# Graph attention, layer 0: edge weights as the stationary operand, features and factor in 65 moving columns, a bank of PSUM for each tile of nodes

## The chip, the cores and the metric

The kernel runs on one core of a Trainium2 chip. The metric is the time of one execution on the device in microseconds (us); the time of a kernel is the median of its runs. One more execution is taken with the hardware profiler, and all views of the profile come from that one.

## What is computed

Two layers on a graph of 3327 nodes with 256 features each. The change touches layer 0, an attention with 4 heads of 64 features:

```python
support = (inputs @ weight).reshape(n, H, OUT_F).transpose(1, 0, 2)
f1 = jnp.einsum('hno,ho->hn', support, weight_u[..., 0])
f2 = jnp.einsum('hno,ho->hn', support, weight_v[..., 0])
w = jax.nn.leaky_relu(f1[:, None, :] + f2[:, :, None], NEG_SLOPE)
e = jnp.where(mask, jnp.exp(neg - m), 0.0)      # mask: adj_mat != 0
attn = e / denom                                # denom: sum of e over the sources
out = jnp.einsum('hnm,hmo->hno', attn, support) + bias + inputs @ proj_w.T + proj_b
```

`inputs` is the input, normalized and cut off at zero; the result is added to the input. So each node gets, for each head, a weighted sum of the features of its sources (65 numbers: 64 features and the sum of the weights that they are divided by). Layer 1 then makes two steps with a dense attention of which only the largest probabilities are kept, and products with the adjacency; it is the longer part of the kernel and stays as it is but for small matters named below.

## The kernel before

All data are f32. The nodes are 26 tiles of 128 (the last has 127). The exponential of a leaky ReLU of a sum is written as a product: the weight from source m to target n is, up to a factor that cancels in the division, `max(cf[m], factor[n]) * adj[m, n]` times `eas[m]`, where `cf`, `eas` and `factor` are exponentials of f1 and f2 made once for each node.

Layer 0 goes over four **blocks** of target nodes (three of 8 tiles, that is 1024 nodes, and one of 255 nodes), and in each block over the 26 tiles j of sources: 104 **steps**. A step does this:

- SP loads a tile of the transposed adjacency `at` three steps ahead (`load_adj`), and POOL's queue stores it once more (`adj_r`, for layer 1).
- DVE makes the weights of each head in one instruction, `w = max(factor, cf) * at` (`weigh`, L560), 128 x 1024. Seven buffers of `w` lie between DVE and PE. The factors lie spread over all partitions, in the tiles `xf0` of layer 1's graph, which are free until then, and for the last block in `cb_end`.
- PE sums over the sources into PSUM. The features `sup` (already multiplied by `eas`) are the stationary operand, 64 columns for a head, and the weights `w` move, 512 columns to a matmul; two heads run side by side in two halves of the array (`sum_features`, L568). The sum of the weights is made apart, with `eas` broadcast to 32 stationary columns, four heads side by side (`sum_weights`, L578). For 1024 nodes that takes six banks of PSUM: two pairs of heads and the sums, each of 2 x 512 columns. An f32 matmul shows in the trace as two weight loads and two matmuls.

In block 0, PE also makes the features of tile j + 10 in step j, while there are any (`turn` L366: two transposes; `features` L377, L379, L381: f1, f2, and 512 columns of features and projection); the first ten tiles are made ahead of the loop. `take` (L410 to L417, DVE) multiplies the features by `eas`. `spread` writes the exponentials of f2 for four tiles at a time to memory and loads them back, broadcast to all partitions, on SP's queue.

At a block's end the six banks are copied to `ot` (L649, ACT and DVE in turn), targets in the columns. The tiles of a finished block (`Out`) then go through seven small stages beside the steps of the next block, three steps apart, listed by step in `on_pe` and `on_dve`: `divide` (L427, three transposes that bring the targets to the partitions), `normalize` (L435 to L454: the division, the residual in four instructions L441, the layer norm), `turn` L463, `keys` L473, `take_keys`, `graph` L496 and `take_graph` L507. Each takes one of the two banks that the sums leave free. The last block's tiles go through the same behind the loop, after the mean of the keys (L262).

The order of the instructions on PE, DVE, ACT and POOL is the order in which the program is written (`in_traced_order`). `load_graph` (L221) loads the graph's tiles from memory between the two steps of layer 1, on POOL's queue, four tiles to a load.

Of the kernel before, what the change touches and what calls it, by code (L numbers as in the profile page):

```python
# [21 lines left out]
P = 128  # L22
D = 256
DC = D // P
H = 4
# [29 lines left out]
def kernel(  # L55
# [25 lines left out]
    HB = 8  # L81

    def rows(i):
        return min(P, N - i * P)

# [84 lines left out]
    def hi_and_lo(qk, p, i, s):  # L170

        pn, at = rows(i), centres[:, s : s + 1]
        if i == 0:
            nc.vector.tensor_reduce(at[DA:], p[DA:, :32], AX.X, ALU.add)
            nc.vector.tensor_scalar(at[DA:], at[DA:], -1.0 / 32, None, ALU.mult)
        nc.scalar.activation(qk[:, 0, :pn], p[:, :pn], AF.Identity, bias=at)
        yield
        nc.vector.scalar_tensor_tensor(
            qk[:, 1, :pn], p[:, :pn], at, qk[:, 0, :pn].bitcast(FP), ALU.add, ALU.subtract
        )  # L180
# [25 lines left out]
    def new_graph(pool):  # L206


        return [
            pool.tile([P, min(HB, NT - c), 2 * DX - 2], FR, tag=f"xf{c}", name=f"xf{c}")  # L210
            for c in range(0, NT, HB)
        ]

    def ones_of_graph(xf, c0, c1):
        b = c0 // HB
        nc.gpsimd.tensor_copy(
            xf[b][:, c0 - b * HB : c1 - b * HB, D:DX],
            one.unsqueeze(2).to_broadcast([P, c1 - c0, DX - D]),
        )

    def load_graph(pool, s):  # L221
        xf = new_graph(pool)
        for g in range(0, NT, 4):
            b = g // HB
            if s == 0:
                ones_of_graph(xf, g, min(g + 4, NT))
            for t0, t1 in ((g, min(g + 4, NF)), (max(g, NF), min(g + 4, NT))):
                if t0 < t1:
                    n0, n1 = t0 * P, min(t1 * P, N)
                    p = min(P, n1 - n0)  # L230
                    for v in range(2):
                        move_rows(
                            nc.gpsimd,
                            xf[b][:, t0 - b * HB : t1 - b * HB, v * DX : v * DX + D].bitcast(FP),
                            xf_d[s][n0:n1, v].rearrange("(t p) d -> p t d", p=p), p,
                        )
        return xf
# [54 lines left out]
    with ExitStack() as l0:  # L292
# [38 lines left out]
        sup = p0.tile([P, NT, D], FP, name="sup")  # L331
        cf = p0.tile([P, NT, H], FP, name="cf")
        eas = p0.tile([P, NT, H], FP, name="eas")
# [5 lines left out]

        cb_end = p0.tile([P, H, N - (NT - 1) // HB * HB * P], FP, name="cb_end")  # L340
# [32 lines left out]
        def features(i, k):  # L373
# [8 lines left out]
            if i % 4 == 0:  # L382
                made["ef"] = pa.tile([H, 4, P], FP, tag="ef", name="ef", bufs=1)
            nc.scalar.activation(eas[:, i], f1, AF.Exp, scale=SLOPE)
            nc.scalar.activation(cf[:, i], f1, AF.Exp, scale=1.0 - SLOPE)
            nc.scalar.activation(made["ef"][:, i % 4], f2, AF.Exp, scale=SLOPE - 1.0)
            if i % 4 == 3 or i == NT - 1:
                spread(i // 4 * 4, i + 1, made["ef"])
            made[i] = pw

        def spread(t0, t1, ef):

            n0, n1 = t0 * P, min(t1 * P, N)
            nc.sync.dma_start(
                out=f2_d[:, n0:n1], in_=ef.rearrange("h t n -> h (t n)")[:, : n1 - n0]
            )
            b = t0 // HB
            for h in range(H):
                src = f2_d[h, n0:n1]
                if b == (NT - 1) // HB:  # L400
                    nc.sync.dma_start(out=cb_end[:, h], in_=src.partition_broadcast(P))
                else:
                    nc.sync.dma_start(
                        out=xf0[b][:, t0 - b * HB : t1 - b * HB, h * P : (h + 1) * P].bitcast(FP),
                        in_=src.partition_broadcast(P).rearrange("q (t n) -> q t n", n=P),
                    )

        def take(i):
            pw = made.pop(i)
            nc.vector.tensor_tensor(  # L410
                sup[:, i].rearrange("p (h o) -> p h o", h=H),
                pw[:, 0].rearrange("p (h o) -> p h o", h=H),
                eas[:, i].unsqueeze(2).to_broadcast([P, H, O]), ALU.mult,
# [6 lines left out]
        class Out:  # L420
            def __init__(r, i, ot, t0):
                r.i, r.pn, r.n0, r.ot, r.t0 = i, rows(i), i * P, ot, t0

            def divide(r, k):
                r.pt = bank(k, [P, HP + 1, P])
                for v in range(HP + 1):
                    nc.tensor.transpose(  # L427
                        r.pt[: r.pn, v, :], r.ot[:, v, r.t0 : r.t0 + r.pn], ident
                    )

            def normalize(r):
                pn, i, pt = r.pn, r.i, r.pt
                rden = small.tile([P, H], FP, tag="rden", name="rden")

                nc.vector.tensor_scalar(rden[:pn], pt[:pn, HP, ::QP], 1.0 / BIG, None, ALU.max)  # L435
                nc.vector.reciprocal(rden[:pn], rden[:pn])
                x1 = pa.tile([P, D], FP, tag="x1", name="x1")
                for h in range(H):
                    hs = slice(h * O, (h + 1) * O)
                    q0 = (h % 2) * O  # L440
                    nc.vector.scalar_tensor_tensor(  # L441
                        x1[:pn, hs], pt[:pn, h // 2, q0 : q0 + O], rden[:pn, h : h + 1],
                        res[:pn, i, hs], ALU.mult, ALU.add,
                    )
# [47 lines left out]
            def graph(r, k):  # L492
# [6 lines left out]
                nc.scalar.copy(xf0[i // HB][:pn, i % HB, :D], pu[:pn, 0])  # L499
# [4 lines left out]
            def take_graph(r):  # L504
                pn, n0, i = r.pn, r.n0, r.i
                xc = xf0[i // HB][:, i % HB]
# [10 lines left out]
        CH = HB * P  # L517
        HP = H // 2
# [32 lines left out]
        def weigh(j, at, b, cn, *heads):  # L551
            pj = rows(j)
            for h in heads:
                ws[h] = w = pa.tile([P, CH], FP, tag="w", name="w", bufs=7)
                if cn == CH:
                    cb = xf0[b][:pj, :, h * P : (h + 1) * P].bitcast(FP)
                    a, o = (t[:pj].rearrange("p (t n) -> p t n", n=P) for t in (at, w))
                else:
                    cb, a, o = cb_end[:pj, h], at[:pj, :cn], w[:pj, :cn]
                nc.vector.scalar_tensor_tensor(o, cb, cf[:pj, j, h : h + 1], a, ALU.max, ALU.mult)  # L560

        def sum_features(accs, j, p):
            pj = rows(j)
            for m, acc in enumerate(accs[p]):
                mn = min(512, cn - 512 * m)
                for q in range(2):
                    h = 2 * p + q
                    nc.tensor.matmul(  # L568
                        acc[q * O : (q + 1) * O, :mn], sup[:pj, j, h * O : (h + 1) * O],
                        ws[h][:pj, 512 * m : 512 * m + mn], start=(j == 0), stop=(j == NT - 1),  # L570
                    )

        def sum_weights(accs, j):
            pj = rows(j)
            for m, acc in enumerate(accs[HP]):
                mn = min(512, cn - 512 * m)
                for h in range(H):
                    nc.tensor.matmul(  # L578
                        acc[h * QP : (h + 1) * QP, :mn],
                        eas[:pj, j, h : h + 1].to_broadcast([pj, QP]),  # L580
                        ws[h][:pj, 512 * m : 512 * m + mn], start=(j == 0), stop=(j == NT - 1),
                    )
# [3 lines left out]
        def load_adj(b, j):  # L586
            c0, pj = b * CH, rows(j)
            cn = min(CH, N - c0)
# [3 lines left out]
        NB = (N + CH - 1) // CH  # L592
# [6 lines left out]
        for step, (b, j) in enumerate(order):  # L599
            c0 = b * CH  # L600
            cn = min(CH, N - c0)
            if j == 0:
                ws = {}
                half = range((cn + 511) // 512)
                accs = [[bank(len(half) * p + m, [P, 512]) for m in half] for p in range(HP + 1)]
# [17 lines left out]
            sum_features(accs, j, 0)  # L623
# [4 lines left out]
            sum_features(accs, j, 1)  # L628
            if b == 0 and i + 1 < NT:
                turn(i + 1, 6)  # L630
            sum_weights(accs, j)
# [12 lines left out]
            ot = pa.tile([P, HP + 1, CH], FP, tag="ot", name="ot", bufs=1)  # L644
            copies = (nc.scalar.copy, nc.vector.tensor_copy)
            for p in range(HP + 1):
                for m, acc in enumerate(accs[p]):
                    mn = min(512, cn - 512 * m)
                    copies[(p + m) % 2](ot[:, p, 512 * m : 512 * m + mn], acc[:, :mn])  # L649
# [3 lines left out]
            outs = [Out(c0 // P + t, ot, t * P) for t in range((cn + P - 1) // P)]  # L653
            if b < NB - 1:
                last = b == NB - 2
                for k, r in enumerate(outs):
                    a = step + 1 + 3 * k
                    ka, kb, kc = ((3, 4)[k % 2], (5, 6)[k % 2], 7) if last else (6, 7, 6)
                    g = a + 5
                    for when, f in (  # L660
                        (a, lambda r=r, ka=ka: r.divide(ka)),
                        (a + (3 if last else 2), lambda r=r, kb=kb: r.turn(kb)),
                        (a + (4 if last else 3), lambda r=r, kb=kb: r.keys(kb)),
                        (g, lambda r=r, kc=kc: r.graph(kc)),
                    ):
                        on_pe.setdefault(when, []).append(f)
                    for when, f in (
                        (a + 1, r.normalize),
                        (a + (5 if last else 4), r.take_keys),
                        (g + 1, r.take_graph),  # L670
# [3 lines left out]
        for k, r in enumerate(outs):  # L674
            r.divide(k)
# [6 lines left out]
        for k, r in enumerate(outs):  # L682
            r.graph(k)
            r.take_graph()

# [24 lines left out]
    def graph(i, s, xf, ends):  # L710
# [5 lines left out]
        for g in range(NG):  # L716
# [21 lines left out]
            for n, (w, c) in enumerate(todo):  # L738
                begin, end = g == 0 and n == 0, g == NG - 1 and n == len(todo) - 1
                xc = xf[c // HB][: rows(c), c % HB]  # L740
# [29 lines left out]
    class Rows:  # L770
# [54 lines left out]
        def guess(r):  # L825
# [31 lines left out]
            for j in (0, 2):  # L857
                g.tensor_scalar(r.at[:pn, j : j + 1], ssum, TOP_P * (1 - MARGIN), None, ALU.mult)
# [557 lines left out]
```

## Time and profile before

| | |
|---|---|
| time, median of 3 runs | 2210.81 us (2210.72 to 2212.17) |
| the profiled execution's own time | 2213.91 us |
| its span, first to last instruction | 2211.7 us |
| granted clock of TensorE, mean | 0.975 |
| PE busy | 2015.5 us, 91% of the span |
| PEld (weight loads) busy | 1394.6 us, 63% |
| DVE busy | 1690.6 us, 76% |
| ACT busy | 1297.6 us, 59% |
| POOL busy | 706.8 us, 32% |
| L560, weights on DVE | 312 instructions of 1277 ns on average |
| L568, sums of features on PE | 1456 rows, 342.5 us busy |
| L578, sums of weights on PE | 1456 rows, 166.5 us busy |

PE is TensorE's matmul, PEld its weight load, which runs beside it; DVE, ACT, POOL and SP are the vector, scalar, GpSimd and sync engines. A view of slices cuts the span into 40 equal parts, each digit being the busy share in tenths. Timelines give the start, the length, the engine, the line of the kernel, the operation, "output<-inputs", the shapes and the count of instructions that were merged into the row; in brackets stands the idle time before them and what ended it. Matmuls are pipelined and their ends are modelled, so the distance of two starts says more than a length. Groups give busy time and the mean length of one in ns.

### The profile page before, as it was taken

Reading aid. Unit: us, or ns where it says so; the run is one execution under the profiler, and the core shown is the slowest. Engines: PE = TensorE matmul, PEld = TensorE weight load, DVE = VectorE, ACT = ScalarE, POOL = GpSimd, SP = SyncE. Lnnn points to the kernel's source line nnn. Section 1 sums busy time; section 2 is a strip of 40 time slices with the busy share of each in tenths; the row PEclk is TensorE's granted clock in tenths of the full one; section 3 lists DMA queues with packets and bytes.
Section 4 is the critical chain, followed back from the end, with each engine's and each line's share of the span. In section 5 each row is a group of like instructions: output and inputs, shape, how many; then the busy total and the mean of one; then the engine's idle time right before and its main releaser. Section 6 shows DMA issues by size and latency. Waiting matters only on the chain. (4 is left out here: it accounts for less than half of the span.)

```text
span 2211.7 us, 34340 instructions
## 1 busy us (share of the span) xinstructions
PE 2015.5 (91%) x11474; PEld 1394.6 (63%) x11474; DVE 1690.6 (76%) x3996; ACT 1297.6 (59%) x2016; POOL 706.8 (32%) x1827
## 2 busy tenths in 40 slices
PE   6999999999997799999999999865999999999997
PEld 3333233233234678888878888754888888888886
DVE  4777888788784678777777777744788888888885
ACT  2110001001113978888888888718898899999982
POOL 2320133223232332222222222214444444444441
PEclk9999999999998799999999999988999999999998
DMA  5445465566454333333333333455333343433330
GB/s 170 147 168 181 164 199 190 190 210 205 152 171 135 83 82 92 95 95 96 96 91 96 96 94 95 115 153 163 84 94 100 94 103 96 112 97 96 93 81 19
DMA packets 319569, 270.60 MB, mean 122 GB/s; under 512 B 30168, under 2 KB 293335, under 8 KB 319256
## 3 DMA queue, kind: packets, MB, share of 16 engines
q1 hardware_dynamic: 303480, 216.03, 36.0%
q0 software_dynamic: 14736, 51.62, 6.5%
q8 instruction: 92, 1.51, 0.3%
q14 instruction: 93, 0.76, 0.1%
q10 hardware_dynamic: 1168, 0.67, 0.1%
HBM read 177.79 MB, written 88.62 MB: 120 GB/s over the span
## 5 line engine op out<-in xcount | busy, mean ns | idle before, releaser
L879 ACT ACTIVATE junk<-lg,at 128x3327 fp8e4<-128x3327 f32 (+1 forms) x208 | 637.9, 3067 | 5.0 <-POOL at L845 2.7
L560 DVE SCALAR_TENSOR_TENSOR w<-xf,cf,at 128x1024 f32<-128x1024 f32 (+1 forms) x312 | 382.0, 1277 | 56.4 <-PE pt L578 56.4
L741 PE MATMUL accr<-xf,adjt 128*128 128x258 f32 (+3 forms) x1352 | 365.9, 304 | 18.7 <-DMA adjt<-adj_r 18.5
L568 PE MATMUL pt<-w,sup 128*64 128x512 f32 (+3 forms) x1456 | 342.5, 579 | 10.4 <-DVE w L560 8.5
L742 PE MATMUL accr<-xf,adjt 128*128 128x256 f32 (+1 forms) x1352 | 339.5, 284 | 0.0
L1018 PE MATMUL acca<-res,wt 128*128 128x256 f32 (+2 forms) x1352 | 324.0, 382 | 0.6 <-ACT wt L1007 0.6
L1018 PE MATMUL acca<-xa,wt 128*128 128x256 f32 (+2 forms) x1352 | 316.4, 383 | 0.1
L997 PE MATMUL pt<-ident,e 128*128 128x128 f32 (+1 forms) x1352 | 208.3, 282 | 81.8 <-DVE e L984 52.4
L741 PEld LDWEIGHTS accr<-xf,adjt 128*128 128x128 f32 (+1 forms) x1352 | 259.7, 192 | 30.1 <-DMA adjt<-adj_r 19.9
L1018 PEld LDWEIGHTS acca<-xa,wt 128*128 128x128 f32 (+2 forms) x1352 | 252.1, 192 | 32.4 <-ACT wt L1007 0.5
L1018 PEld LDWEIGHTS acca<-res,wt 128*128 128x128 f32 (+2 forms) x1352 | 247.4, 192 | 30.1 <-ACT wt L1007 1.2
L742 PEld LDWEIGHTS accr<-xf,adjt 128*128 128x128 f32 (+1 forms) x1352 | 260.2, 192 | 4.6
L798 PE MATMUL pg<-k_sb,q 128*128 128x512 f32 (+2 forms) x728 | 237.4, 428 | 21.3 <-ACT lg L809 12.0
L997 PEld LDWEIGHTS pt<-ident,e 128*128 128x128 f32 (+1 forms) x1352 | 164.7, 146 | 144.7 <-ACT wt L1007 46.4
L819 POOL TENSOR_SCALAR sc<-sc 128x1 f32<-128x1 f32 (+1 forms) x156 | 30.8, 224 | 662.0 <-ACT sc L817 662.0
L568 PEld LDWEIGHTS pt<-w,sup 128*64 128x64 f32 (+1 forms) x1456 | 96.2, 136 | 222.3 <-issue 149.7
L945 DVE MAX8 v<-lg 128x8 f32<-128x416 f32 (+2 forms) x416 | 209.9, 577 | 0.0
L1007 ACT COPY wt<-pt 128x512 f32<-128x512 f32 (+3 forms) x286 | 148.1, 520 | 100.1 <-PE pt L997 93.2
L936 DVE SCALAR_TENSOR_TENSOR lg<-e,th 128x3327 f32<-128x3327 f32 (+1 forms) x52 | 191.1, 3675 | 2.2 <-ACT th L929 2.2
L984 DVE SCALAR_TENSOR_TENSOR e<-e,vm 128x3327 f32<-128x3327 f32 (+1 forms) x52 | 191.4, 3680 | 0.9
L821 ACT ACTIVATE e<-lg,sc 128x3327 f32<-128x3327 f32 (+1 forms) x52 | 159.8, 3074 | 25.2 <-PE pt L997 22.9
L578 PE MATMUL pt<-w,eas 128*32 128x512 f32 (+3 forms) x1456 | 166.5, 568 | 0.0
(179 smaller groups left out, 2615.5 us busy)
## 6 DMA issues: line engine op xcount, KB each, us to landing
adjt<-adj_r SPq DMA_DIRECT2D x300, 256.0 KB, 3.1
at<-in_adj_t_dram SPq DMA_DIRECT2D x75, 512.0 KB, 3.7
adj_r<-at POOLq DMA_DIRECT2D x75, 512.0 KB, 4.8
qk_d<-qk SPq DMA_DIRECT2D x50, 128.0 KB, 2.4
q<-qk_d SPq DMA_DIRECT2D x100, 64.0 KB, 2.4
xf_d<-xf SPq DMA_DIRECT2D x50, 128.0 KB, 2.8
xf_d<-hl SPq DMA_DIRECT2D x25, 256.0 KB, 2.1
xf<-f_d SPq DMA_DIRECT2D x24, 256.0 KB, 4.9
```

The costliest lines, as they stand in the source:

```text
L560: nc.vector.scalar_tensor_tensor(o, cb, cf[:pj, j, h : h + 1], a, ALU.max, ALU.mult)
L568: nc.tensor.matmul(acc[q * O : (q + 1) * O, :mn], sup[:pj, j, h * O : (h + 1) * O], ws[h][:pj, 512 * m : 512 * m + mn], start=(j == 0), st ...
L578: nc.tensor.matmul(acc[h * QP : (h + 1) * QP, :mn], eas[:pj, j, h : h + 1].to_broadcast([pj, QP]), ws[h][:pj, 512 * m : 512 * m + mn], sta ...
L741: nc.tensor.matmul(acc[:pn, :dx], w, xc[:, :dx], start=begin, stop=False)
L742: nc.tensor.matmul(acc[:pn, :D], w, xc[:, DX:], start=False, stop=end)
L798: nc.tensor.matmul(r.pg[p][:pn, :mn], r.q[:, v, :pn], k_sb[:, m0 : m0 + mn], start=(v == 0), stop=(v == 1),)
L879: nc.scalar.activation(junk[:pn], r.lg[:pn, :N], AF.Exp, bias=r.at[:pn, 4:], accum_out=r.g[:pn], saturate=False,)
L936: nc.vector.scalar_tensor_tensor(r.lg[:pn, :N], e, r.th[:pn], e, ALU.is_lt, ALU.mult, accum_out=r.below[:pn])
L945: nc.vector.max(r.v8[:pn, q], r.lg[:pn, q * w : min((q + 1) * w, N)])
L984: nc.vector.scalar_tensor_tensor(e, e, r.vm[:pn, 1:], e, ALU.is_ge, ALU.mult, accum_out=kept[:pn])
L997: nc.tensor.transpose(r.pt[g][: rows(c), j, : r.pn], r.e[: r.pn, c * P : c * P + rows(c)], ident[: r.pn, : r.pn],)
L1018: nc.tensor.matmul(r.acc[: r.pn], wt[: rows(c), j, : r.pn], xa[: rows(c), c, :], start=(c == 0), stop=(c == NT - 1),)
```

## The change

The operands of the sums change places. `w` becomes the stationary operand, 128 sources by 128 targets, and 65 columns move: the 64 features of the head and, as the 65th, `eas`. So the targets come out in the partitions, a bank of PSUM holds the 4 x 65 sums of one tile of targets, and neither the sums of the weights apart nor the transposes of `divide` are there any more. Six banks hold the sums of six tiles, so the blocks are now five: four of 6 tiles and one of two (`BLOCKS`), and what was spread and loaded four tiles at a time goes by three (`CHUNKS`).

```diff
-    HB = 8
+    BLOCKS = ((0, 6), (6, 12), (12, 18), (18, 24), (24, NT))
+    CHUNKS = tuple((t, min(t + 3, NT)) for t in range(0, NT, 3))
...
-        sup = p0.tile([P, NT, D], FP, name="sup")
+        sup = p0.tile([P, NT, H, O + 1], FP, name="sup")
...
-            nc.scalar.activation(eas[:, i], f1, AF.Exp, scale=SLOPE)
+            nc.scalar.activation(sup[:, i, :, O], f1, AF.Exp, scale=SLOPE)
...
+        def factors(b):
+
+            w = (BLOCKS[b][1] - BLOCKS[b][0]) * P
+            t = xf0[b].rearrange("p t d -> p (t d)")[:, : H * w]
+            return t.bitcast(FP).rearrange("p (h n) -> p h n", h=H)
...
-            def divide(r, k):
-                r.pt = bank(k, [P, HP + 1, P])
-                for v in range(HP + 1):
-                    nc.tensor.transpose(
-                        r.pt[: r.pn, v, :], r.ot[:, v, r.t0 : r.t0 + r.pn], ident
-                    )
...
-                for h in range(H):
-                    hs = slice(h * O, (h + 1) * O)
-                    q0 = (h % 2) * O
-                    nc.vector.scalar_tensor_tensor(
-                        x1[:pn, hs], pt[:pn, h // 2, q0 : q0 + O], rden[:pn, h : h + 1],
-                        res[:pn, i, hs], ALU.mult, ALU.add,
-                    )
+                nc.vector.tensor_tensor(
+                    x1[:pn].rearrange("p (h o) -> p h o", h=H), sums[:, :, :O],
+                    rden[:pn].unsqueeze(2).to_broadcast([pn, H, O]), ALU.mult,
+                )
+                nc.vector.tensor_add(x1[:pn], x1[:pn], res[:pn, i])
...
-        CH = HB * P
-        HP = H // 2
+
+        CH = max(t1 - t0 for t0, t1 in BLOCKS) * P
...
+                nc.vector.scalar_tensor_tensor(
+                    w[:pj, :cn], factors(b)[:pj, h, :cn], cf[:pj, j, h : h + 1], at[:pj, :cn],
+                    ALU.max, ALU.mult,
+                )
+
+        def sum_up(accs, j, cn, *heads):
+
             pj = rows(j)
+            for h in heads:
+                for t, acc in enumerate(accs):
+                    mn = min(P, cn - t * P)
                     nc.tensor.matmul(
+                        acc[:mn, h], ws[h][:pj, t * P : t * P + mn], sup[:pj, j, h],
+                        start=(j == 0 and h == 0), stop=(j == NT - 1 and h == H - 1),
                     )
...
-                accs = [[bank(len(half) * p + m, [P, 512]) for m in half] for p in range(HP + 1)]
+                accs = [bank(t, [P, H, O + 1]) for t in range(b1 - b0)]
...
-            sum_features(accs, j, 0)
+            sum_up(accs, j, cn, 0, 1)
             if b == 0 and i < NT:
                 features(i, 7)
             for f in on_pe.pop(step, ()):
                 f()
-            sum_features(accs, j, 1)
+            sum_up(accs, j, cn, 2)
             if b == 0 and i + 1 < NT:
                 turn(i + 1, 6)
-            sum_weights(accs, j)
+            sum_up(accs, j, cn, 3)
...
-            ot = pa.tile([P, HP + 1, CH], FP, tag="ot", name="ot", bufs=1)
+            outs = []
             copies = (nc.scalar.copy, nc.vector.tensor_copy)
...
+            for t, acc in enumerate(accs):
+                mn = min(P, cn - t * P)
+                sums = pa.tile([P, H, O + 1], FP, tag="ot", name="ot", bufs=CH // P)
+                copies[t % 2](sums[:mn], acc[:mn])
+                outs.append(Out(b0 + t, sums))
```

The stages of a finished tile are listed anew for six tiles to a block: normalize in the step where divide was, and the others one to two steps earlier than before. The graph's tiles `xf` follow the blocks of six, their loads the chunks of three. Two more small edits lie outside: the mean of the first keys is taken over 16 columns in place of 32 (`hi_and_lo`), and one of two constants in `guess` (POOL) is a little larger.

## The prediction

> **What bounds the kernel now.** I read the share of each engine in 40 slices first, since the change touches one stage only.
>
> ```profile
> PE   6999999999997799999999999865999999999997
> DVE  4777888788784678777777777744788888888885
> ```
>
> A slice is 55.3 us (2211.7 / 40). PE stands at 9 from the second to the twelfth, with DVE at 7 or 8: layer 0's sums end near 680 us, and PE looks like their bound. The stages say it more exactly. I cut the stretch at the starts of L560 (weights), which marks each block's first step, and at L262, after the last sums. Columns: length, then busy time and instructions of PE, PEld, DVE, ACT, POOL, clock, DMA share, GB/s.
>
> ```profile
> 52.40:254.10 201.70, 199.80 (x1055) 64.54 (x1054) 153.43 (x180) 20.58 (x81) 39.42 (x52) 0.99 0.51 165
> 254.10:429.50 175.40, 172.94 (x936) 53.24 (x936) 147.33 (x190) 15.58 (x41) 51.81 (x59) 0.99 0.59 195
> 429.50:604.20 174.70, 171.96 (x936) 53.20 (x936) 147.01 (x189) 16.79 (x45) 51.55 (x59) 1.00 0.55 182
> 604.20:683.80 79.60, 75.24 (x521) 30.12 (x522) 61.42 (x187) 16.54 (x45) 27.81 (x57) 1.00 0.54 162
> ```
>
> These 631.4 us are the four blocks before. PE is busy 99% in the first three, DVE 76 to 84%. The third view is PE's timeline over two plain steps of block 0:
>
> ```profile
> 209.87 3.65 PE L568 MATMUL pt<-w,sup 128*64 128x512 f32 x16
> 213.46 1.92 PE L578 MATMUL pt<-w,eas 128*32 128x512 f32 x16
> 215.31 3.65 PE L568 MATMUL pt<-w,sup 128*64 128x512 f32 x16
> ```
>
> A step takes 215.31 - 209.87 = 5.44 us. An f32 matmul shows as two rows (two passes). The 16 rows of L568 run in pairs (64 columns of the array each), those of L578 in fours, so the step is 8 + 4 = 12 passes of 512 columns at 0.43 us, or 5.15, and 0.3 for changing between the two shapes. DVE needs 4 x 1.196 = 4.78 of it (L560 start to start) and waits 0.57 for PE. So PE bounds, and DVE is 12% behind.
>
> **What a new pass costs.** The changed program holds 2704 matmuls of 65 moving columns (26 source tiles x 4 heads x 26 target tiles), so 5408 passes, each with its own load of 128 f32 columns of weights. No row has that pair; these enclose it (start, length of the whole run, count at the end):
>
> ```profile
> 30.04 0.53 PEld L377 LDWEIGHTS pt<-wuv,hT 128*128 128x128 f32 x4
> 1705.24 1.07 PE L997 MATMUL pt<-ident,e 128*128 128x128 f32 x8 [0.92 <-DVE e L984]
> 1700.15 1.89 PE L1018 MATMUL acca<-xa,wt 128*128 128x256 f32 x8
> ```
>
> - L377 moves 4 columns only. Four loads take 0.53, one alone 0.192 by its group: (0.53 - 0.19) / 3 = **0.112 us** a pass. So few columns stream for next to no time: this is the pace of a 128x128 f32 load.
> - L997 moves 128 columns behind the same load: (1.07 - 0.27) / 7 = 0.114, and 0.109 between starts inside the run.
> - L1018 moves 256: (1.89 - 0.38) / 7 = 0.216, which is the 0.43 us of 512 columns halved. The next load starts 2 ns after the matmul starts and adds nothing: load and matmul overlap, and the longer one sets the pace.
>
> 65 columns stream for 65/256 of 0.213 = 0.054 us, half of the load. So the pass waits for the load: I take 0.112, from L377, which has the same load and a stream shorter than it. From below 0.109 (L997). From above 0.118, the pace of L741/L742 (256 columns in 0.28-us rows that start 0.12 apart), where load and stream both take about 0.107 and get in each other's way.
>
> The page "TensorE: Matmul & The Clock Gate" of the Trainium skill, section "LDWEIGHTS (loading the stationary operand)", makes a load P / 1.2 ns for P columns, whatever the rows: 107 ns here, an estimate that speaks against the change and would make the passes 27 us cheaper in sum than mine. The same page's Part 3 says that a load overlaps matmuls in flight only where the row group differs; L1018's 0.216 has the same rows in both and shows overlap, so there the trace decides.
>
> **The sum, from 52.4 us to the end of the sums.**
> - Sums: 5408 x 0.112 = 606. Before: 26 x (3 x 5.44 + 1.77) = 470, 1.77 being the unladen step of 255 columns (609.22 to 610.99, starts of L560). So +136 on the path. A step of six tiles costs 48 x 0.112 = 5.4 us, as much as one of eight before: same price, a quarter fewer nodes.
> - Features in 16 steps of block 0: 8.94 - 5.44 = 3.50 before. Their passes alone make 4 x 0.112 + 4 x 0.109 + 4 x 0.43 + 2 x 0.109 = 2.8; without shape changes around them I put 3.0, so 48 and not 56.
> - The finished tiles that run beside the next block, 24 as before (four times six, three times eight), at turn 0.22 + keys 0.44 + graph 1.72 = 2.4, with gaps 2.6: 62. Before, divide (three transposes, 0.33) and shape changes around each made about 3.25: 78.
> - Block ends: DVE's copy of the last bank waits for PE's last pass, and the next block's L560 stand behind it in DVE's queue; PE waits for them. Copy about 0.4, one weight instruction of 768 columns 0.93 ((1.196 - 0.395) / 769 = 1.042 ns a column, from the 1024 and 255 rows), latencies 0.2, and about 1.1 more when normalize stands ahead of head 2: 2.6 x 4 = 10. Before, the step 13.42 us at 416.12 held the last graph and six copies of 0.6 to 0.7, some 6 more than a plain step: 19 for three.
> - Last block: PE 16 x 0.112 = 1.8 a step, DVE 1.58 and its share of the tiles' work; I add 4 for waits on both, against 8 before (laden steps took 9.17 in three, PE's own sum was 8.8, eight tiles).
> - Start and last copies: 2, as before less the flush of the last graph.
>
> 606 + 48 + 62 + 10 + 4 + 2 = 732 against 631: **+101 us**.
>
> Costed at nothing: DVE's 520 weight instructions in place of 416 (104 x (4 x 0.929 + 0.395) = 428 against 425 before) lie under PE, 3.7 in a 5.4 us step; without PE as cover they would be the bound, as in the first rival. The four L441 of 0.19 become two of 0.42 on DVE: +0.1 a tile, under PE. DMA moves the same bytes of adjacency in five pieces, in a longer stretch than the one at 165 to 195 GB/s. The spread of the factors issues nine groups of five on SP rather than seven; ACT's exponential into the single ef buffer waits for its store every third tile, with the copy of hT behind it, and PE for that: a store is 0.27 us of issue and some 2 to landing, features come 8 us apart in the loop, so only the opening can feel it: 0 to 2 us. Between the layers POOL issues four more loads of the graph; there each issue already waits about 1 us for the one ahead (340 GB/s), the bytes are equal, and I put 0, within 5 either way. Layer 1's plan stays as it is but for one constant on POOL, the same number of instructions.
>
> The profiled execution took 2213.9 (span 2211.7, 2.2 around it), so 2315 on its scale; it lies 3.1 above the median 2210.8, and 2210.8 + 101 = **2312**.
>
> **The rivals.**
> 1. *Faster: the pass goes at its 65 columns.* If loads of f32 weights came quicker than L377 shows, a pass would take 65/128 of 0.107 + 0.0025 = 0.057: 308 us in all, PE 420. DVE would bound: 428 + 84 (its 509 busy less 425) + about 25 of waits = 537, 94 less than 631: 2117. The sign turns at (606 - 101) / 5408 = 0.093 us a pass. For it: nothing loads f32 weights under a stream of 65 columns. Against: 104 passes of L377 with 4 columns, whose loads come no faster than 0.11.
> 2. *Slower by far: the load isn't hidden* behind so short a matmul: 0.112 + 0.054 = 0.166, +292: 2604. Against it: L1018 and L997 overlap.
> 3. *Load and stream disturb each other* as in L741/L742: 0.118, +32, and a wait of each head's first load for DVE of up to 0.03 (520 of them, 15): 2345 to 2360.
> 4. *The clock falls*, since the array streams half of the time only. Granted clock is 0.80 where PE is busy 70% (700 to 750 us) and 1.00 at 99%. With half the clock throughout it would be +600: about 2900. The loads keep PE occupied without gaps over 3 us, so I give it little.
>
> The page "TensorEngine Tiling (Array Packing)", section "Performance Considerations", advises to swap stationary and streaming where the RHS is at most 64 wide, together with column tiling; here the RHS is 65 wide and no columns are tiled, and no row shows that form.
>
> **How the numbers follow.** Forecast (0.109 to 0.114 and the small terms) 0.79; third rival 0.12; first 0.05; second 0.03; the fourth or something near no change 0.01. Bounds: 0.109 takes 16 off, the gaps in features and tiles another 10: 2285. 0.118 and the heads' waits add 47: 2360. What lies outside is some 0.1 to 0.2. Within 0.2%, about what measurement can tell from no change, I put 0.01; faster 0.05; slower 0.94.
>
> **What would show it.** PE at 9 in all slices up to some 780 us. The new rows' loads 0.11 apart, 48 passes in 5.4 us. Plain steps of block 0 near 5.4, laden ones 8.4. DVE waiting on PE between steps, longer than 0.57. No three transposes a tile. I'm wrong if loads come under 0.093 apart, if steps show DVE back to back, or if the clock drops there.

## The result, and the profile after

The changed kernel takes 2384.28 us (median of 4 runs, 2382.59 to 2386.07) against 2211.21 for the kernel before: 1.0782 times as long, 95% interval 1.0764 to 1.0801. That is 173 us slower where 101 were forecast, and 24 above the upper end of the range. The profiled execution spans 2384.2 us against 2211.7.

The page of the changed kernel, its slices of 59.6 us:

```profile
PE   6999999999999977999999999986699999999987
DVE  4667477477477746787777777784588888888885
...
PEclk9999599599599788999999999998799999999998
```

The clock of the kernel before, in its slices of 55.3 us:

```profile
PEclk9999999999998799999999999988999999999998
```

PE is busy for longer, up to the fourteenth slice, as forecast. The line that was not forecast is the clock: before, it stood at 9 in the first twelve slices, up to 663 us of layer 0's 684; now it falls to 5 three times, once after the start of each of blocks 1 to 3, and to 7 in the last block. DVE's dips to 4 lie in the three slices of 5. The blocks (from the first weight instruction of each to the next, and the last up to the mean of the keys) show how much; columns as in the prediction:

```profile
51.30:244.50 193.20, 191.71 (x1472) 170.18 (x1470) 125.34 (x181) 19.91 (x81) 35.48 (x51) 0.97 0.42 136
244.50:422.70 178.20, 176.71 (x1308) 169.40 (x1308) 114.43 (x157) 12.64 (x33) 39.64 (x51) 0.87 0.45 147
422.70:600.90 178.20, 176.61 (x1308) 169.81 (x1308) 114.31 (x157) 12.57 (x33) 39.12 (x51) 0.87 0.44 144
600.90:780.70 179.80, 178.27 (x1308) 171.01 (x1308) 114.33 (x157) 12.57 (x33) 39.66 (x51) 0.86 0.42 136
780.70:857.00 76.30, 73.73 (x476) 66.33 (x476) 57.52 (x155) 11.46 (x31) 24.31 (x50) 0.82 0.49 149
```

These are 805.7 us against 631.4: +174, all of the difference. What lies behind them, layer 1 with the four more loads of its graph, takes 1527 against 1528 us (mean of the keys to the end).

Within block 1 the clock is at a half for 47.8 us and full for the rest:

```profile
247.40:295.20 47.80, 47.80 (x214) 45.57 (x214) 22.20 (x32) 1.94 (x4) 10.89 (x13) 0.50 0.32 109
295.20:422.70 127.50, 127.14 (x1082) 122.03 (x1081) 89.43 (x120) 10.70 (x29) 28.75 (x38) 1.00 0.51 164
```

PE's timeline at the start and at the end of that stretch says what stands there:

```profile
241.81 2.17 PE L563 MATMUL pt<-sup,w 127*128 127x65 f32 x18
245.64 2.70 PE L563 MATMUL pt<-sup,w 128*128 128x65 f32 x19 [1.65 <-DVE w L552]
```

```profile
271.08 20.58 PE L563 MATMUL pt<-sup,w 128*128 128x65 f32 x96
291.46 3.72 PE L493 MATMUL pt<-ug,hT 128*128 128x512 f32 x4
294.97 0.48 PE L460 MATMUL pt<-ident,res 128*128 128x128 f32 x2
295.29 4.91 PE L563 MATMUL pt<-sup,w 128*128 128x65 f32 x43
```

Ahead of the stretch lies the end of a block: PE's last pass starts at 243.7, and the next block's first at 245.6, since DVE must copy a bank and then make weights. In the stretch 96 passes take 20.4 us from start to start (291.46 less 271.08), 0.212 each. It ends with the first matmuls of 512 columns, the first finished tile's graph product in step 4; behind them a pass takes (4.91 - 0.28) / 42 = 0.110. All together, the record of the granted clock has 184 us at half clock in these blocks (10.2, 47.8, 47.8, 51.2, 27.3) and 6.8 in the blocks before the change. Each of these stretches is a whole number of 3.4 us, called a window from here on. Half of the added 177 is 89 us, more than the 72 that were missing from the forecast.

### The profile page after: what moved, and what is told of

Same layout as the page of the kernel before. It is cut to its first block, busy times and chain, and to the rows that moved or that the text cites. A ratio compares the mean times of both kernels' runs of the same rounds, so it can differ in the third digit from the quotient of the medians.

```text
span 2384.2 us, 39418 instructions
## 1 busy us (share of the span) xinstructions
PE 2190.6 (92%) x13892; PEld 1939.3 (81%) x13892; DVE 1706.8 (72%) x4051; ACT 1296.6 (54%) x2018; POOL 716.8 (30%) x1858
## 5 line engine op out<-in xcount | busy, mean ns | idle before, releaser
L563 PEld LDWEIGHTS pt<-sup,w 128*128 128x128 f32 (+2 forms) x5408 | 689.0, 211 | 19.1 <-issue 15.2
L563 PE MATMUL pt<-sup,w 128*128 128x65 f32 (+2 forms) x5408 | 690.3, 294 | 8.3 <-DVE w L552 8.3
L552 DVE SCALAR_TENSOR_TENSOR w<-xf,cf,at 128x768 f32<-128x768 f32 (+2 forms) x520 | 442.6, 904 | 58.0 <-PE pt L563 57.8
L783 PEld LDWEIGHTS pg<-k_sb,q 128*128 128x128 f32 (+1 forms) x728 | 126.0, 194 | 43.8 <-ACT lg L794 16.3
```

What stands on the lines that cost most here:

```text
L552: nc.vector.scalar_tensor_tensor(w[:pj, :cn], factors(b)[:pj, h, :cn], cf[:pj, j, h : h + 1], at[:pj, :cn], ALU.max, ALU.mult,)
L563: nc.tensor.matmul(acc[:mn, h], ws[h][:pj, t * P : t * P + mn], sup[:pj, j, h], start=(j == 0 and h == 0), stop=(j == NT - 1 and h == H - 1),)
L783: nc.tensor.matmul(r.pg[p][:pn, :mn], r.q[:, v, :pn], k_sb[:, m0 : m0 + mn], start=(v == 0), stop=(v == 1),)
```

## The experiments

The theory, made from these lines: the idle time at a block's end halves the clock. The stream of 65 columns, in which the array works only 0.054 of 0.112 us by the prediction's estimate, can keep a full clock, but can't win it back; only a dense stream can. That it keeps the clock shows at the end of block 0, where 504 passes run for 56 us without any other matmul at a clock of 1.00:

```profile
187.60 56.39 PE L563 MATMUL pt<-sup,w 128*128 128x65 f32 x504
```

The rivals: the thin stream loses the clock by itself, idle time or not (theory 2); a fixed delay follows a block's end, whatever PE does (theory 3); or the time goes with the columns streamed, and the clock is only company.

**fill4: four matmuls of 512 columns into the gap at a block's end.**

They go into bank 7, and their result is left unread.

```diff
+        def dense(count, k):
+            pd = bank(k, [P, 512])
+            for n in range(count):
+                nc.tensor.matmul(
+                    pd, ident, sup[:, :2].rearrange("p t h o -> p (t h o)")[:, :512],
+                    start=(n == 0), stop=(n == count - 1),
+                )
...
+            if b < NB - 1:
+                dense(4, 7)
```

> The changed kernel with four matmuls of 512 moving columns into a spare bank between the last sums of a block and the first of the next, where PE otherwise sits idle for some 2.5 us. Their result is not used. Theory 1 (the idle time at a block's end halves the clock, and the 65-column stream, which keeps a full clock, cannot win it back): no half clock after the four block ends, 174 us at half clock become 10 or less, so 2384 - 85 + about 4 = 2303 us. Theory 2 (the 65-column stream is too thin to hold the clock, idle or not; block 0 only holds it through its features): the clock falls some windows later all the same, about 2388. Theory 3 (a fixed delay of some 48 us that follows the copies at a block's end, whatever PE does): about 2388.

Measured: 2309.31 us (2308.77 to 2309.5), ratio 1.0444 (1.0426 to 1.0461). The timeline of PE at the first block's end, now without a gap:

```profile
239.73 3.51 PE L563 MATMUL pt<-sup,w 127*128 127x65 f32 x30
243.08 3.65 PE L571 MATMUL pt<-sup,ident 128*128 128x512 f32 x8
246.56 5.69 PE L563 MATMUL pt<-sup,w 128*128 128x65 f32 x50
```

The pass stays at (5.69 - 0.28) / 49 = 0.110 behind it, no stretch of blocks 1 to 4 is at half clock, and blocks 1 to 3 take 157 us in place of 178 to 180. More work made the kernel 75 us faster. Theories 2 and 3 fall.

**dense4: the same four matmuls behind the gap**, in step 0 after heads 0 and 1.

```diff
+            if b and j == 0:
+                dense(4, 7)
```

> The changed kernel with the four unused matmuls of 512 columns in the first step of blocks 1 to 4, after heads 0 and 1, so behind the idle time and not in it. Theory 1: the clock halves as before, but comes back with these matmuls, about 10 us after a block's start and not at the first tile's graph product some 50 us after it: 38 us less at half clock in three blocks, 15 in the last, or 65 us of time saved, and 4 x 4 to 7 us for the matmuls: about 2340. Theory 2: the clock rises and falls again, 2384 to 2405. Theory 3 (fixed delay): about 2405.

Measured: 2324.46 us (2319.79 to 2329.13). The clock falls at each of blocks 1 to 4 and comes back after one to three windows of 3.4 us (6.8, 10.2, 10.2 and 3.4 us at half). PE's timeline behind the gap:

```profile
246.49 3.80 PE L563 MATMUL pt<-sup,w 128*128 128x65 f32 x24 [1.65 <-DVE w L552]
250.08 6.11 PE L571 MATMUL pt<-sup,ident 128*128 128x512 f32 x8
256.03 5.47 PE L563 MATMUL pt<-sup,w 128*128 128x65 f32 x48
```

The eight rows begin 0.85 apart and end 0.43 apart: the clock came back within them. The gain is 60 us rather than the 44 expected; part of it is that the clock came back sooner, in the last block above all (3.4 us at half, where 12 had been left).

**delay3: the finished tiles three steps later.**

```diff
-                    a = step + 1 + 3 * k
+                    a = step + 4 + 3 * k
```

> The changed kernel with all stages of the finished tiles three steps later, so that the first graph product (512 columns) stands in step 7 of a block and not in step 4. Theory 1 (the dense product is what brings the clock back): three more steps at half clock, 5 us more each in three blocks and about 1 in the last, 2384 + 48 = 2432, and the low stretches are 30 us longer. Theory 3 (a fixed delay): stretches of 48 us as before, 2384. Theory 2: somewhat over 2384, as the clock falls in between anyway.

Measured: 2433.45 us (2432.27 to 2434.64), 49 more than the changed kernel. The stretches at half clock are 78.5, 81.9, 81.9 and 37.5 us long, 30 more in the long blocks, and the first ends with the first graph product again:

```profile
309.73 13.01 PE L563 MATMUL pt<-sup,w 128*128 128x65 f32 x60
322.53 3.30 PE L493 MATMUL pt<-ug,hT 128*128 128x512 f32 x4
325.67 0.38 PE L460 MATMUL pt<-ident,res 128*128 128x128 f32 x2
325.89 4.35 PE L563 MATMUL pt<-sup,w 128*128 128x65 f32 x38
```

So the length is set by when the dense product comes, not by a timer.

**w128, w96, w80: more moving columns.** The columns that follow in memory go along; their sums are left unread. The same edit with three sizes:

```diff
-                        acc[:mn, h], ws[h][:pj, t * P : t * P + mn], sup[:pj, j, h],
+                        acc[:mn, h], ws[h][:pj, t * P : t * P + mn],
+                        flat[:pj, (j * H + h) * (O + 1) : (j * H + h) * (O + 1) + WIDE],
...
```

> The changed kernel with 128 moving columns in place of 65 in each sum: the 63 columns that follow in memory go along, and what they give in PSUM is left unread. A pass then streams for 107 ns, as long as its load. Theory 1 and 2 (clock): the array is busy nearly all the time, a dip at a block's end lasts a window or two, so 2384 - 80 = 2304; with the loads and streams in each other's way (0.118 a pass) 2335. Rival (time follows the columns streamed, the load is hidden or added): 5408 x 63 x 0.83 ns = 283 us more, 2667.

Measured: 2304.21 us (2302.09 to 2305.52), ratio 1.042 (1.0403 to 1.0438). Twice the columns, and 80 us less. The page's clock, and the blocks:

```profile
PEclk9999999999999879999999999998899999999999
```

```profile
53.00:242.00 189.00, 187.51 (x1471) 167.43 (x1470) 125.34 (x181) 19.91 (x81) 35.47 (x51) 1.00 0.43 138
242.00:398.40 156.40, 154.16 (x1308) 147.83 (x1308) 114.08 (x157) 12.57 (x33) 39.74 (x51) 1.00 0.50 167
398.40:554.90 156.50, 154.16 (x1308) 147.83 (x1308) 113.77 (x157) 12.57 (x33) 38.91 (x51) 1.00 0.50 165
554.90:711.40 156.50, 154.16 (x1308) 147.83 (x1308) 113.78 (x157) 12.57 (x33) 39.44 (x51) 1.00 0.47 156
711.40:777.20 65.80, 62.98 (x476) 56.46 (x476) 56.46 (x155) 11.27 (x31) 24.77 (x50) 0.97 0.56 173
```

The counts of instructions are those of the changed kernel, the clock is at 1.00 in four blocks and 0.97 in the last, and the blocks take 724 us in place of 806. A pass stays at 0.112 (134 loads in 15.04 us at the end of block 0). So 82 us of the loss are the clock's, and streaming 63 more columns behind a load costs nothing. Of the 82, 4 lie in block 0: the changed kernel starts it with 10.2 us at half clock, after 0.98 us of idle time, and this run does not.

> The changed kernel with 96 moving columns in place of 65 (31 neighbours go along, their sums are left unread). The array streams 0.080 of 0.112 us, 71%, against 48% with 65 columns and 95% with 128. If the stream alone can win the clock back from some share on, and that share lies under 71%: as with 128 columns, 2304 us. If it must be nearly full: as with 65, 2384. In either case the pass stays at 0.112 at full clock.

Measured: 2307.41 us (2307.09 to 2307.74). After three block ends the clock is at half for one window of 3.4 us, and back.

> The changed kernel with 80 moving columns (15 neighbours go along, unread): the array streams 60% of the pass. 2304 us if that is enough to win the clock back, 2384 if not, and between them if it comes back late. I expect about 2384, as nothing so far shows recovery under a thin stream.

Measured: 2383.95 us (2383.32 to 2384.57), with stretches at half clock of 47.8, 47.8, 51.2 and 27.3 us as with 65. In these runs the stream won the clock back where the array works 71% of the time, and not at 60%, both shares being the estimates of the expectations.

**fill1: one matmul in the gap.**

> The changed kernel with one unused matmul of 512 columns (0.86 us) at each block's end in place of four, so that some 1.7 us of the idle time are left. Theory 1, if any idle time of more than a microsecond closes the clock: 2384, low stretches of some 48 us as before. If the clock looks at a window's share of work: it stays at full where the remaining gap is a small enough part, in all or some of the blocks, 2305 to 2345.

Measured: 2376.43 us (2374.98 to 2377.88). The clock falls in all four blocks, for 41.0, 44.4, 44.4 and 20.5 us. The timeline shows what idle time is left at the end of block 0, twice less than a microsecond:

```profile
243.85 1.08 PE L571 MATMUL pt<-sup,ident 128*128 128x512 f32 x2
245.66 2.86 PE L563 MATMUL pt<-sup,w 128*128 128x65 f32 x24 [0.74 <-DVE w L552]
249.29 0.88 PE L563 MATMUL pt<-sup,w 128*128 128x65 f32 x6 [0.77 <-DVE w L552]
```

With so thin a stream around it, that is enough. With 128 columns the whole gap stands at every block's end, but the clock stays full at the first three and is at half for one window of 3.4 us at the fourth, where PE is idle for 1.00 and 1.50 us with eight passes between. The lines at the first and the fourth:

```profile
243.14 2.92 PE L566 MATMUL pt<-sup,w 128*128 128x128 f32 x24 [1.65 <-DVE w L555]
714.63 7.24 PE L566 MATMUL pt<-sup,w 128*128 128x128 f32 x48 [1.50 <-DVE w L555]
```

So it isn't the length of a gap alone. A share of work within a window may be the rule, but no run shows its limits beyond the widths tried here.

**w128fill4: both.**

> 128 moving columns and four unused matmuls at each block's end together. If both act through the clock alone, the second has nothing left to do: 2304 us as with 128 columns, plus up to 3 for matmuls that outlast the idle time. If filling the gap has a worth of its own, about 2295.

Measured: 2309.06 us (2304.7 to 2309.39), 2 above what was allowed for the first case (2307) and not below w128. Filling the gap has no worth of its own; the two act through the same thing.

**cols64, cols32: the load made shorter.** With the clock settled, the forecast's own price was left: the 0.112 of a pass is its load of 128 columns. Each sum is split into matmuls for 64 target nodes, or for 32 in cols32 (with 32 in both places where the edit has 64), in their own columns of the array; nothing is left out.

```diff
-                    nc.tensor.matmul(
-                        acc[:mn, h], ws[h][:pj, t * P : t * P + mn], sup[:pj, j, h],
+                    for q0 in range(0, mn, 64):
+                        q1 = min(q0 + 64, mn)
+                        nc.tensor.matmul(
+                            acc[q0:q1, h], ws[h][:pj, t * P + q0 : t * P + q1], sup[:pj, j, h],
...
```

> The changed kernel with each sum split into two halves of 64 target nodes, which use 64 columns of the array each, as the old sums of features did (there the loads of two halves start 6 ns apart and the matmuls run side by side). If the time of a load goes by its columns and the two halves load side by side, a pair takes the stream's 0.054 or the load's 0.053 in place of 0.112: PE's sums fall to some 310 us, DVE becomes the bound (428 for the weights and 84 besides, and waits), layer 0's blocks take some 540 us and the kernel 2117 to 2150, faster than both kernels. If the loads of the halves go one after the other, or each instruction has a floor of its own near 0.05: 0.112 a pair as before, 2300 (the clock kept by denser rows) to 2384.

Measured: **2125.04 us** (2124.41 to 2125.45), ratio 0.9618 to the kernel before (0.9602 to 0.9634): faster than both, by 84 and 259 us. The first three blocks:

```profile
52.40:196.40 144.00, 141.05 (x2719) 105.90 (x2718) 122.59 (x181) 19.76 (x81) 35.49 (x51) 0.98 0.56 181
196.40:311.30 114.90, 103.65 (x2556) 89.69 (x2556) 111.92 (x159) 12.39 (x33) 43.75 (x51) 0.96 0.70 229
311.30:425.00 113.70, 102.14 (x2556) 87.66 (x2556) 111.35 (x156) 12.39 (x33) 43.75 (x51) 0.98 0.69 228
```

Twice the rows on PE in less time: two loads start 6 or 7 ns apart and a pair takes 0.058 us. In blocks 1 and 2 DVE is now busy 97 and 98%, the bound that the first rival had named. The clock still falls, mostly at the block ends, but under the denser rows it is back after at most 6.8 us: 30.7 us at half in all five blocks.

The page "TensorEngine Tiling (Array Packing)" of the Trainium skill, section "Performance Considerations", recommends the swap of the operands together with column tiling for a right-hand side of up to 64 columns. These runs agree with the whole of it at 65 columns: the swap alone loses 173 us, with two column tiles it wins 84.

> The same in four quarters of 32 target nodes. If loads and matmuls of the quarters run side by side: the stream's 0.054 binds, 2117 to 2150, as with halves. If each of the matmuls costs a floor in issue, twice as many show it: 2200 to 2400, above the run with halves.

Measured: 2312.52 us (2310.59 to 2314.45). Four quarters together also take 0.057, but PE stands still between bursts. The waits between 52 and 720 us (us in total, times, longest):

```profile
PEld pt L565 <- issue: 235.9, 176, 4.3
PE pt L565 <- issue: 188.8, 119, 4.2
```

"issue" is a wait for nothing that the profile shows, up to 4 us at a time. The clock is at half for 95 us of the blocks, in stretches of 3.4 to 10.2, but that is worth 48 us at most, of the 187 that lie between cols32 and cols64. Twice as many instructions as in cols64 pass through PE's queue; that their supply is the limit is likely but wasn't tried.

## Why the prediction was wrong

Its direction and its main price were right. One step failed: rival 4, the clock, was given almost no chance ("The loads keep PE occupied without gaps over 3 us, so I give it little") and only one price, half clock throughout. The gap at the block ends, which the sum itself contains as 2.6 us, was enough, and the thin stream behind it kept the clock low until the next dense product, for 174 us behind the four ends. The cost was 82 us (805.7 less 724.2), put down as 0. The prediction did name a falling clock as one of the signs that it is wrong.

The trace of before held a hint. At the end of its block 0 PE is idle for 2.10 us, and the clock answered at once; under the old sums, dense in two halves of the array, it was back after one window:

```profile
255.54 4.29 PE L568 MATMUL pt<-w,sup 128*64 128x512 f32 x8 [2.10 <-DVE w L560]
255.80:259.20 3.40, 3.40 (x7) 0.98 (x6) 3.40 (x4) 0.00 (x0) 0.00 (x0) 0.50 0.02 5
```

The end of its block 1 has an even longer gap, and behind it the clock stays at 1.00, so a gap alone doesn't decide it there either:

```profile
430.96 3.04 PE L568 MATMUL pt<-w,sup 128*64 128x512 f32 x8 [2.48 <-DVE w L560]
```

I read the clock by blocks (0.99) and asked whether it would fall, not what would bring it back. The page "TensorE: Matmul & The Clock Gate", section "Why this matters for your kernels", asks for no idle gaps over some 3 us; here, with a thin stream around it, a gap of 1.65 closed it, and so did two of some 0.75, so the measurement decides.

The other steps, by the run with 128 columns, which has the same instructions at full clock:

- *A pass at 0.112, from L377.* In the changed kernel, at full clock:

```profile
225.12 0.86 PEld L563 LDWEIGHTS pt<-sup,w 128*128 128x128 f32 x7
```

  (0.86 - 0.19) / 6 = 0.112. Right, and neither 0.118 nor 0.166: rivals 2 and 3 are out, and at 128 columns, where load and stream are about as long as each other, the pass is still 0.112.
- *A plain step at 5.4, a laden one of block 0 at 8.4:* 5.36 and 8.32.
- *The sum to the end of the blocks, 732:* 724. For each of blocks 1 to 3 it makes 26 x 5.376 + 6 x 2.6 + 2.6 = 158.0, where 156.5 were measured; that is 4.5 of the eight too many, and the rest lies in the last block and small terms. The forecast of 2312 for a full clock compares with 2304 (w128) and 2309 (fill4).
- *DVE under PE's cover, 3.7 in a step of 5.4:* right; it waits 0.32 us for PE before each weight instruction of a plain step.
- *The four more loads between the layers at nothing:* right, 1527 against 1528.
- *First rival, DVE as the bound, 2117:* cols64 came near it by another way, 2125, with 547 us of blocks against 537.

What stays open: the exact rule by which the clock falls and returns, and what holds PE back in cols32.

## What to carry to other kernels

When a change makes TensorE's stream thinner (short moving operand behind a long weight load), price two things: the pass by the longer of load and stream, and the clock by what comes after each gap. Here a stream that kept the array at work 48 or 60% of the time stayed in the state that it found, so each of the four gaps cost until the next dense matmul. Dense filler in the gap, or unread columns that are free behind a load, gave nearly all of that time back (75 and 80 us). Where the load is the longer part, try to split the stationary operand over two halves of the array before giving the swap up; here that won 259 us.

## What the hardware showed that I had not expected

- A stream in which the array works 48% of the time held the full clock for 56 us, yet ran at half clock for as long as 82 us (delay3) without raising it. With 71% it rose within one window of 3.4 us; with 60% it did not.
- 63 more moving columns made the kernel 80 us faster, and four unused matmuls at each block's end 75 us.
- Two weight loads of 64 f32 columns side by side take half of one load of 128: 0.058 against 0.112 us a pass. Four of 32 take 0.057 in bursts, with stalls of up to 4 us between them.
